# Graph network layers on one core: a memset behind every gather, and the next gather queued behind it

## The chip, the core and the metric

The kernel runs on one core of one Trainium2 chip. The metric is the device time of one launch in microseconds, as a median over runs without the profiler. A profile is one further execution, recorded by the hardware profiler; it takes longer than a plain run, as the table below shows.

## The reference

There are 12,500 nodes with 64 features and 400,000 edges, sorted by their target node `dst`. The first layer transforms nodes and edges and sums messages over the edges; the second multiplies twice by the normalised adjacency. Layer norms with residuals stand around both.

```python
x_t = mlp2(x, W1n, b1n, W2n, b2n)            # 12500 x 64
e_t = mlp2(edge_attr, W1e, b1e, W2e, b2e)    # 400000 x 64
msgs = x_t[src] * e_t * dp_scale
out = x + segment_sum(msgs, dst) * res_w
x = layernorm(x + norm(out) * gamma + beta)
# second layer: edges (src, dst) and self loops, weights deg^-1/2 on both ends
for _ in range(2):
    h = segment_sum(edge_weight * h[dst], src)
x = layernorm(x + h @ W.T + b)
```

## The kernel before

The edges are cut into 3125 chunks of 128 (one edge to a partition), and twelve chunks make a group `q`; there are 261 groups, taken from the last to the first.

Before the main loop the kernel computes `x_t` and stores it in the DRAM table `xt_tab`. For every group, `gathers` (L545) then issues one indirect DMA for each chunk from POOL (L553): it fetches the 128 rows `x_t[src]`, of 256 bytes each, into the tile `xg`. The pool of `xg` has four buffers, so gathers run up to four groups ahead of their use; a gather into a reused buffer waits until the product that read it is done. `load_ea` loads the edge features of the group over SP's queue.

Each group passes through these steps: `hidden` (L574, two products on PE, ScalarE and VectorE behind them), `message` (L588, L590 on PE, then the product with the gathered rows on VectorE, L598, in two halves), `level1` (L613, L623, L632: sums within the group) and `level2` (L642, L652: sums into a ring of node windows). `nodes` finishes windows of nodes with layer norms.

Beside this the same loop builds the adjacency as counts, in blocks: `adjacency` makes one-hot rows on VectorE (L795, L836), multiplies them on PE (L839), converts the sums on ScalarE (L853) and stores them (L862). Its edges come by indirect DMAs from POOL too (`fetch`, L738). `hop1` multiplies finished parts of the adjacency on PE (L1033, L1045, L1163).

After the loop comes the second hop. Part of it is dense on PE (L1138, L1149); the rest is sparse: POOL gathers rows (`sp_fetch`, L1357), PE multiplies them (L1375), and POOL scatters the sums by accumulating indirect DMAs into four tables (`sp_add`, L1388). POOL then adds the tables (L1515) and the last layer norm follows.

The order of instructions on each engine is set by a scheduler that simulates the timeline. The kernel gives it priorities: edge steps are traced at high priority, and pieces of adjacency and hop 1 are handed out between them in fixed shares. `tc.issue_after(ins)` adds an edge without a semaphore: what is traced in the block stands behind `ins` in its engine's queue.

Of the kernel before, what the change touches and what calls it, by code (L numbers as in the profile page):

```python
# [11 lines left out]
F32 = mybir.dt.float32  # L12
# [9 lines left out]
P = 128  # L22
# [162 lines left out]
def tile_fast(  # L185
# [42 lines left out]
    nc = tc.nc  # L228
    xt_tab = tc.dram_tile([NPAD, D], F32, name="xt_tab")
# [25 lines left out]
    CHK_SLOT, CHK_SG, CHK_Q = 2 * NSEG, 2 * NSEG + NSBP, 2 * NSEG + NSBP + len(SGS)  # L255

    const = ctx.enter_context(tc.tile_pool(name="const", bufs=1))
    main = ExitStack()
    idxp = main.enter_context(tc.tile_pool(name="idxp", bufs=2))
    xgp = main.enter_context(tc.tile_pool(name="xgp", bufs=4))  # L260
# [2 lines left out]
    with tc.tile_pool(name="srch", bufs=2) as srch, tc.tile_pool(  # L263
        name="srch1", bufs=1
# [40 lines left out]
        for k in range(NSBP):  # L305
            nc.gpsimd.indirect_dma_start(
                out=run[:, k, :],
                out_offset=None,
                in_=runs,
                in_offset=bass.IndirectOffsetOnAxis(ap=blki[:, k : k + 1], axis=0),  # L310
# [234 lines left out]
    def gathers(q):  # L545
        si, _ = seg[q // SEGQ]
        xg = xgp.tile([P, QC, D], F32, name="xg")
        real = min(QC, NCH - q * QC)
        if real < QC:
            nc.vector.memset(xg[:, real:, :], 0.0)  # L550
        for i in range(real):
            c = (q % SEGQ) * QC + i
            nc.gpsimd.indirect_dma_start(  # L553
                out=xg[:, i, :],
                out_offset=None,
                in_=xt_tab,
                in_offset=bass.IndirectOffsetOnAxis(ap=si[:, c : c + 1], axis=0),
            )
        xgs[q] = xg

    last_load = [None]

    def load_ea(q):
        t = eap.tile([P, SCC * P], F32, name="eat")
        last_load[0] = nc.sync.dma_start(t, ea[q]).ins
        eas[q] = t
# [620 lines left out]
    def take(q):  # L1187
        k = q // SEGQ
        if k not in seg:
            load_seg(k)  # L1190
        gathers(q)
        load_ea(q)
# [29 lines left out]
    for t in range(NQ + 3):  # L1222
# [18 lines left out]
        for f in units:  # L1241
# [3 lines left out]
            while a_live and a_spent < a_goal:  # L1245
                c = next(a_gen, None)
# [5 lines left out]
            while h_live and h_budget > 0:  # L1252
                try:
                    c = next(h_gen)
# [944 lines left out]
def build(nc, fast, general, params, out, **kw):  # L2199
    with tile.TileContext(nc, schedule_with_timeline_sim=True) as tc, ExitStack() as ctx:  # L2200
        fp = ctx.enter_context(tc.tile_pool(name="flag", bufs=1))
        flag = fp.tile([1, 1], I32, name="flag")
        tile_fast(tc, flag, *fast, *params, out, **kw)
        again = nc.values_load(flag, min_val=0, max_val=1)
        with tc.If(again > 0):
            tile_general(
                tc, *general, *params, out.rearrange("(p j) d -> p j d", j=NJ)
            )
# [27 lines left out]
```

## Time and profile before

| | before |
|---|---|
| median of 3 runs | 5303.93 us (5302.65 to 5309.74) |
| profiled execution | 7307.16 us, its span 7305.0 us |
| mean granted TensorE clock in the profile | 0.801 |
| PE busy | 5406.8 us, 74% of the span |
| VectorE busy | 3330.4 us, 46% |
| ScalarE busy | 2331.9 us, 32% |
| POOL busy | 3925.7 us, 54% |
| gathers (L553) | 3125, mean 1009 ns, from 93.0 to 6288.2 us |
| scatter-adds (L1388) | 389, mean 1558 ns, after the gathers |

Busy times are those of the profiled execution. A row of the costliest groups names the line, engine, operation, the tile written and those read, the count, busy time and the mean of one, and then the engine's idle time just before these instructions with what ended most of it. "issue" there means that the engine waited for nothing that the profile shows. A row of the timeline gives start and duration in microseconds, and in brackets the idle time before.

### The profile page before, as it was taken

The numbers are of one execution on the slowest core, as the hardware profiler recorded it, in microseconds if no ns is written. First come the engines' busy times: TensorE is split into PE (matmuls) and PEld (weight loads), VectorE is DVE, ScalarE is ACT, GpSimd is POOL, SyncE is SP. The second block draws the span as 40 slices with busy tenths as digits, with TensorE's granted clock in tenths as the row PEclk, the third lists the DMA queues.
The fourth block names the chain that finished last, engine by engine and source line by source line (L and its number), as shares of the span: only waits on it lengthen the run. The fifth ranks groups of instructions, "written<-read, shape, count | busy, mean of one in ns | idle before, by whom it ended". The sixth has DMA issues, their size and how long they took to land.

```text
span 7305.0 us, 91998 instructions
## 1 busy us (share of the span) xinstructions
PE 5406.8 (74%) x31510; PEld 2960.0 (41%) x31510; DVE 3330.4 (46%) x10617; ACT 2331.9 (32%) x7808; POOL 3925.7 (54%) x3677
## 2 busy tenths in 40 slices
PE   4666877778687776868777777787776776789992
PEld 2333443344343343434333334444344444534441
DVE  4545444545545545454454555555456543510003
ACT  1555444534433333333333343232222111210000
POOL 6555555554554544454444555555555454268885
PEclk6777888788788787778877888888788786599996
DMA  3534444434334333434343433333322222299884
GB/s 93 141 83 96 99 104 92 89 87 97 82 84 88 83 85 76 86 81 92 69 93 79 89 84 82 84 80 76 74 66 51 49 67 72 85 212 203 192 177 104
DMA packets 1258944, 698.98 MB, mean 96 GB/s; under 512 B 607516, under 2 KB 1191424, under 8 KB 1257440
## 3 DMA queue, kind: packets, MB, share of 16 engines
q1 hardware_dynamic: 1097552, 566.52, 31.2%
q0 software_dynamic: 160912, 126.49, 11.9%
q8 instruction: 249, 4.08, 0.2%
q14 instruction: 231, 1.89, 0.1%
HBM read 493.05 MB, written 199.62 MB: 95 GB/s over the span
## 4 chain that ended last, share of the span: by engine, by line
PE 60%; issue 12%; another core or an unknown queue 12%; DVE 5%; ACT 4%; POOL 4%; DMA 2%; SPq 0%; DVEq 0%; POOLq 0%; ACTq 0%
PE pa L839 15%; PE hacc_p L1033 10%; PE hacc_p L1045 6%; PE pw L574 6%; PE pe L590 5%; PE pl L623 5%; POOL hop_tab L1388 4%; PE pc L1163 3%; ACT stage L853 3%; PE acc L1138 3%; PE ring L652 2%; DVE oh L836 2%; PE pe L588 2%; PE acc L1149 1%
## 5 line engine op out<-in xcount | busy, mean ns | idle before, releaser
L553 POOL DMA_INDIRECT xg<-xt_tab,si x3125 | 3154.7, 1009 | 2995.7 <-issue 880.8
L836 DVE TENSOR_SCALAR oh<-iota_b,colT 128x391 bf16<-128x391 bf16 x6054 | 1707.7, 328 | 1710.0 <-PE pa L839 791.5
L853 ACT ACTIVATE stage<-pa 128x391 fp8e4<-128x391 f32 x3077 | 1507.9, 504 | 1930.0 <-PE pa L839 871.8
L839 PE MATMUL pa<-oh,koh 128*64 128x391 bf16 (+2 forms) x6054 | 1484.9, 410 | 726.7 <-issue 417.1
L839 PEld LDWEIGHTS <-koh 128*64 128x64 bf16 (+2 forms) x6054 | 718.7, 178 | 1188.6 <-issue 955.2
L1033 PE MATMUL hacc_p<-at,gp 128*128 128x512 fp8e4 (+1 forms) x2425 | 902.2, 432 | 202.6 <-ACT hev L1084 99.3
L1388 POOL DMA_INDIRECT hop_tab<-tot,first x389 | 605.9, 1558 | 119.4 <-issue 114.3
L574 PE MATMUL pw<-eat,w1ab 128*128 128x384 f32 x1044 | 545.3, 609 | 168.6 <-ACT z L575 85.6
L853 ACT ACTIVATION_READ_ACCUMULATOR stage<-pa 128x1 f32 x3077 | 642.4, 209 | 0.0
L1045 PE MATMUL hacc_p<-at,gp 128*64 128x512 fp8e4 (+1 forms) x2425 | 609.6, 448 | 10.5 <-issue 10.1
L590 PEld LDWEIGHTS pe<-w,z 128*128 128x128 f32 x3132 | 529.0, 230 | 123.7 <-issue 104.5
L590 PE MATMUL pe<-w,z 128*128 128x128 f32 x3132 | 553.5, 316 | 33.3 <-issue 33.1
L575 ACT ACTIVATE z<-pw,b 128x384 f32<-128x384 f32 x522 | 304.6, 584 | 628.8 <-remote 176.3
L623 PE MATMUL pl<-msg,oh 128*32 128x65 f32 x6264 | 419.1, 242 | 77.8 <-issue 65.0
L1045 PEld LDWEIGHTS <-gp 128*64 128x64 bf16 x2425 | 159.5, 113 | 780.3 <-issue 776.2
L652 PE MATMUL ring<-tot,oh 128*128 128x65 f32 x1096 | 205.5, 317 | 306.7 <-ACT tot L632 195.7
L1138 PE MATMUL acc<-at,gp 128*128 128x512 fp8e4 (+1 forms) x1900 | 429.6, 380 | 0.0
L623 PEld LDWEIGHTS pl<-msg,oh 128*32 128x32 f32 x6264 | 301.1, 120 | 236.5 <-issue 166.5
L598 DVE TENSOR_TENSOR msg<-pe,xg 128x384 f32<-128x384 f32 x522 | 287.9, 552 | 232.4 <-remote 107.0
L613 DVE TENSOR_TENSOR oh<-iota_f,rel 128x384 f32<-128x384 f32 x261 | 145.0, 556 | 539.5 <-remote 321.6
L1033 PEld LDWEIGHTS <-gp 128*128 128x128 bf16 x2425 | 179.5, 101 | 420.2 <-issue 399.0
L795 DVE TENSOR_TENSOR koh<-iota_k,keyT 128x1024 bf16<-128x1024 bf16 (+6 forms) x393 | 337.8, 860 | 0.0
(212 smaller groups left out, 4132.7 us busy)
## 6 DMA issues: line engine op xcount, KB each, us to landing
adj<-stage SPq DMA_DIRECT2D x390, 391.0 KB
at<-adj SPq DMA_DIRECT2D x97, 896.0 KB
at<-adj SPq DMA_DIRECT2D x144, 512.0 KB
eat<-in_eaq_dram SPq DMA_DIRECT2D x261, 192.0 KB
xg<-xt_tab,si POOLq DMA_INDIRECT x3125
at<-adj SPq DMA_DIRECT2D x120, 256.0 KB
at<-adj SPq DMA_DIRECT2D x24, 832.0 KB
at<-adj SPq DMA_DIRECT2D x24, 768.0 KB
```

What stands on the lines that cost most here:

```text
L553: nc.gpsimd.indirect_dma_start(out=xg[:, i, :], out_offset=None, in_=xt_tab, in_offset=bass.IndirectOffsetOnAxis(ap=si[:, c : c + 1], axis=0),
L574: nc.tensor.matmul(pw, w1ab[:, h, :], eas[q], start=True, stop=True)
L590: nc.tensor.matmul(pe[:, :, c, :], z[:, h, c * P : (c + 1) * P], w2, start=False, stop=(c == SCC - 1),)
L623: nc.tensor.matmul(pl[REL * s : REL * (s + 1), :], oh[:, s * SCC + c, :], m[:, s * SCC + c, :], start=(c == 0), stop=(c == SCC - 1), tile_ ...
L652: nc.tensor.matmul(ring[:, w % RING, :], oh[:, (w - lo) * P : (w - lo + 1) * P], tot, start=False, stop=False, skip_group_check=True,)
L836: nc.vector.tensor_scalar(oh, iota_b, colT[:, i % P : i % P + 1], None, op0=ALU.is_equal)
L839: nc.tensor.matmul(pa[rows, :], koh.pop(i), oh, start=(j == 0), stop=(j == caps[g] - 1), tile_position=(0, rows.start),)
L853: nc.scalar.activation(stage[:, u, :], pa, AF.Identity, saturate=True, accum_out=sums[:, u : u + 1],)
L1033: nc.tensor.matmul(acc[:, :w], gp[:kk, lo + i, 0:2, :].rearrange("p t d -> p (t d)"), t[:kk, i, :w], start=start, stop=False, skip_group_c ...
L1045: nc.tensor.matmul(acc[D * h : D * (h + 1), :w], gp[:kk, lo + i, 2, :], t[:kk, i, :w], start=False, stop=False, skip_group_check=True, til ...
L1138: nc.tensor.matmul(acc[:, :w], gp[:kk, wi, 0:2, :].rearrange("p t d -> p (t d)"), t[:kk, wi - lo, :w], start=first and n == 0, stop=False, ...
L1388: nc.gpsimd.indirect_dma_start(out=hop_tab[(q * QC + i) % HT], out_offset=bass.IndirectOffsetOnAxis(ap=first[:, q - Q0, i : i + 1], axis=0 ...
```

## The change

A tile `pause` of 128x128 f32 is added, which nothing reads. After every gather POOL sets it to zero. The memset is queued behind its gather, and the next gather behind the memset; other POOL work (the fetches) is not tied to it. The memsets all write one tile, so each also waits for the memset before it, on POOL's own semaphore.

```diff
     const = ctx.enter_context(tc.tile_pool(name="const", bufs=1))
+    pause = const.tile([P, P], F32, name="pause")
     main = ExitStack()
...
         for i in range(real):
             c = (q % SEGQ) * QC + i
-            nc.gpsimd.indirect_dma_start(
-                out=xg[:, i, :],
-                out_offset=None,
-                in_=xt_tab,
-                in_offset=bass.IndirectOffsetOnAxis(ap=si[:, c : c + 1], axis=0),
-            )
+            with tc.issue_after(last_pause[0]) if last_pause else ExitStack():
+                got = nc.gpsimd.indirect_dma_start(
+                    out=xg[:, i, :],
+                    out_offset=None,
+                    in_=xt_tab,
+                    in_offset=bass.IndirectOffsetOnAxis(ap=si[:, c : c + 1], axis=0),
+                ).ins
+            with tc.issue_after(got):
+                last_pause[:] = [nc.gpsimd.memset(pause, 0.0).ins]
         xgs[q] = xg
 
     last_load = [None]
+    last_pause = []
```

## The prediction

> **What bounds the kernel now.** I began with the page's busy shares and its forty slices, to see which engines are candidates and where the stages change; then the costliest groups; then POOL's timeline, because the edit touches POOL alone.
>
> ```profile
> PE 5406.8 (74%) x31510; PEld 2960.0 (41%) x31510; DVE 3330.4 (46%) x10617; ACT 2331.9 (32%) x7808; POOL 3925.7 (54%) x3677
> ...
> L553 POOL DMA_INDIRECT xg<-xt_tab,si x3125 | 3154.7, 1009 | 2995.7 <-issue 880.8
> L1388 POOL DMA_INDIRECT hop_tab<-tot,first x389 | 605.9, 1558 | 119.4 <-issue 114.3
> ```
>
> The first line makes POOL look half idle. The second says what its idle time is: before the 3125 gathers 2995.7 us pass, of which 880.8 us wait for nothing. The timeline shows that this part is a fixed price.
>
> ```profile
> 1024.42 0.94 POOL L553 DMA_INDIRECT xg<-xt_tab,si  x1 [0.30 <-issue]
> 1025.67 1.72 POOL L553 DMA_INDIRECT xg<-xt_tab,si  x1 [0.30 <-issue]
> 1027.70 0.94 POOL L553 DMA_INDIRECT xg<-xt_tab,si  x1 [0.30 <-issue]
> ...
> 1034.00 0.94 POOL L553 DMA_INDIRECT xg<-xt_tab,si  x1 [0.30 <-issue]
> 1043.64 1.01 POOL L553 DMA_INDIRECT xg<-xt_tab,si  x1 [8.70 <-DVE oh L836]
> ```
>
> Columns are start, duration, and in brackets the idle time before. Twelve gathers of a group follow each other with 0.30 us between them, never less; then POOL waits 8.70 us until an xg buffer is free. So a gather takes POOL 0.30 + 1.009 (its mean) = 1.31 us, and the rest of the 2995.7 us is waiting for buffers: in the profiled execution POOL has room.
>
> That room belongs to the profile. The profiled execution took 7307.16 us (span 7305.0), the median of the runs is 5303.93, so recording added 2003 us. It did not add it to POOL:
>
> ```profile
> 3000.73 0.94 POOL L553 DMA_INDIRECT xg<-xt_tab,si  x1 [0.30 <-issue]
> 3000.79 0.22 PE L623 MATMUL pl<-msg,oh 128*32 128x65 f32 x1 [1.18 <-issue]
> ...
> 3001.98 0.95 POOL L553 DMA_INDIRECT xg<-xt_tab,si  x1 [0.30 <-issue]
> ...
> 3003.62 0.38 PE L623 MATMUL pl<-msg,oh 128*32 128x65 f32 x2 [1.09 <-issue]
> ```
>
> PE, waiting for nothing, starts a small matmul only every 0.7 to 1.4 us, while POOL keeps its 1.25 us. The chain that ended last has 12% "issue" of this kind. So I add up POOL as if it never waited for a buffer: 93.0 us until the first gather; 3154.7 + 45.9 us busy in the 3125 gathers and 48 fetches (L738), and 3173 x 0.30 = 952 us between them, 4152 together; 140.3 us of handover before the first g4t (L1357); 875.5 us from there to the span's end, in which 389 scatter-adds run at 1.56 + 0.30 each with hardly a wait; 2.2 us outside the span. That is **5263 us, against a median of 5304**: 41 us of waiting are left. I read POOL as the bound without the profiler. PE is close behind: from back-to-back spacings in the timeline (six L839 products in 1.26 us, six L590 in 0.67, a pair each of L1033 and L1045 in 0.87, L574 0.8 each), its products up to the handover need about 3960 us, an estimate, 15.2 us per group of twelve chunks against POOL's 15.9. That two engines fit the median leaves room for error, which the range takes in.
>
> [...]
>
> **The change, part by part.**
>
> Nothing is removed and no DMA is added. Added are 3125 memsets of 128x128 f32 on POOL, one behind each gather. Each also waits for the memset before it (same tile, POOL's own semaphore); that one ended more than a gather earlier, so the wait should cost nothing. Queued behind each memset are the next gather, or an ed fetch, and whoever waits for those: msg L598 for xg, and the key preparation for ed.
>
> The price is in the start of the trace:
>
> ```profile
> 0.81 0.20 POOL masks.py:197 MEMSET ident<- 128x128 f32 x1 [0.29 <-POOLq L2216]
> 1.06 0.55 POOL L383 IOTA iota_i<- 128x512 int32 x1
> ```
>
> Same op, shape and type; start to next start is 1.06 - 0.81 = 0.25 us. I take **0.25 us** on top of the gather's 1.31, assuming the 0.30 gap remains. Sum: 3125 x 0.25 = 781 us; 5263 + 781 = **6044**, taken as 6040. Per group 12 x 0.25 = 3.0 us: POOL goes from 15.9 to 18.9, above PE's 15.2, so nothing takes the lead from POOL. Set against the profile's own time, the same 781 us fall into the 2996 - 952 = 2044 us of buffer waiting there, 7.8 us per group; a profile of the changed kernel may grow by only 0 to 400 us while the plain runs grow by 730. That cover isn't there without the profiler.
>
> What no row shows is the transition gather to memset to gather. Lower bound: the memset runs inside the 0.30 gap, 0; below nothing, if spacing the gathers also cured their delays, (1009 - 944) x 3125 = -203 us. Upper bound: a full 0.30 gap ahead of the memset too, 0.20 + 0.30 = 0.50[...]: 0.55, or 1719 us. I take 0.25 because tiny POOL instructions at the trace's start follow each other at 0.03 us, so a compute instruction does not itself need a 0.30 gap.
>
> Moved: the scheduler plans anew. In the order of PE's instructions more adjacency products (L839) now stand ahead of the early edge steps: before the 160th of 522 L574 products, 2047 instead of 1585 of 6054; POOL's first ed fetches come after 8 gathers instead of 20. Amounts are the same. With POOL slower this is the fitting order; splitting both orders into nine stretches and taking the slower of PE and POOL in each gives 685 us more instead of 781 at 18.9 against 15.9 per group. I keep 781 less a little, and count 41 us either way for the order. [...]
>
> **The rivals.**
>
> *Hidden in the gap.* [...] For it: memsets at 0.03 us spacing show overlapped dispatch. Against: the gap is as constant as a serial step. Time: 5304 with the order's 41 us either way; partly hidden (0.03 to 0.12 us) 5400 to 5680.
>
> *Switching costs on both sides.* 0.40 to 0.55 us each: 5263 + 1250 to 1719 = 6510 to 6980. For it: the constant gap at each gather. Against: nothing shows it for a memset.
>
> *Faster: spaced gathers stop stalling.* Place: gathers of 1.3 to 1.7 us such as the one at 1025.67, which with the mean cost 203 us in all. [...] It decides only when the memset adds under 0.065 us, so it needs the hidden case too: 5100 to 5290. Against: the scatter-adds run as closely at a steady 1.55.
>
> *POOL isn't the bound after all.* Were the 0.30 gap partly the profiler's, PE would set the time, and of 781 us only what exceeds POOL's slack would show: with 0.15 us less per gather (469 us slack), about 5620.
>
> **How the numbers follow.** Serial memset at 0.15 to 0.36 us, 5700 to 6400: 0.60, time 6040. Switching costs above that: 0.15. Partly hidden or PE-bound, 5315 to 5700: 0.11. Wholly hidden within 0.2% (some 11 us, about what a measurement of this kernel can tell): 0.04. Faster: 0.10. So slower 0.86. The range 5400 to 6750 leaves out the two last cases and the ends of two others, under 2 in 10.
>
> **What would show it.** A row of 3125 memsets near 204 ns on POOL; starts of gathers within a group 1.50 us apart, not 1.25; waiting for buffers before the gathers down by several hundred us; xg named as a releaser of L598 more often; the scatter stage unchanged at 1.86. Starts still 1.25 apart would make the forecast wrong, as would 1.50 apart with plain runs that don't lengthen: then POOL was not the bound.

## The result, and the profile after

The changed kernel takes 5592.91 us in the median (5589.85 to 5597.56, 4 runs) against 5306.84 us for the kernel before (4 runs): a ratio of 1.0538, with a 95% interval of 1.0519 to 1.0556. It is slower by 286 us, where some 736 us had been forecast (6040 less 5304).

The first recorded execution of the kernel before took 7307 us, and recording is not the reason: in one later job all eleven runs of that kernel took 7251 to 7361 us, for a cause that was not looked for, while its second recorded execution, the first experiment below, took 5328 us. So it does not hold here that a profile takes longer than a plain run, and what the change does is read from that second profile and the profile of the changed kernel.

The lines of the page of the changed kernel that answer to those shown of before (busy time and share, then the costliest groups on POOL, with line numbers shifted by the edit):

```profile
PE 4896.7 (88%) x31510; PEld 2774.8 (50%) x31510; DVE 3415.6 (61%) x10617; ACT 2279.8 (41%) x7808; POOL 4714.0 (84%) x6802
...
L555 POOL DMA_INDIRECT xg<-xt_tab,si x3125 | 3238.6, 1036 | 516.7 <-issue 494.8
...
L562 POOL MEMSET pause<- 128x128 f32 x3125 | 710.3, 227 | 1.5
L1393 POOL DMA_INDIRECT hop_tab<-tot,first x389 | 605.2, 1556 | 121.0 <-issue 113.7
```

The memsets are there, 3125 of them at 227 ns. The idle time before the gathers is 516.7 us, which is 0.165 us each, and 494.8 us of it is "issue": POOL hardly waits for a buffer. The scatter-adds (L1393) are as they were. The timeline of POOL shows the new step; the columns are start, duration and, in brackets, the idle time before:

```profile
1002.84 0.22 POOL L562 MEMSET pause<- 128x128 f32 x1
1003.22 0.95 POOL L555 DMA_INDIRECT xg<-xt_tab,si  x1 [0.16 <-issue]
1004.16 0.23 POOL L562 MEMSET pause<- 128x128 f32 x1
1004.55 1.01 POOL L555 DMA_INDIRECT xg<-xt_tab,si  x1 [0.16 <-issue]
1005.56 0.22 POOL L562 MEMSET pause<- 128x128 f32 x1
```

The memset begins as the gather ends, lasts 0.22 us, and the next gather begins 0.16 us after it. From the end of one gather to the start of the next pass 0.38 us, where the kernel before has 0.30. The memset does not come on top of the gap; it lies in it and lengthens it by 0.08 us (from 0.305 to 0.381 us in the median of all gathers of the two traces).

### The profile page after: what moved, and what is told of

It reads as the page before. It is cut to its first block, busy times and chain, and to the rows that moved or that the text cites. A ratio compares the mean times of both kernels' runs of the same rounds, so it can differ in the third digit from the quotient of the medians.

```text
span 5593.3 us, 95026 instructions
## 1 busy us (share of the span) xinstructions
PE 4896.7 (88%) x31510; PEld 2774.8 (50%) x31510; DVE 3415.6 (61%) x10617; ACT 2279.8 (41%) x7808; POOL 4714.0 (84%) x6802
## 4 chain that ended last, share of the span: by engine, by line
POOL 42%; PE 33%; DVE 9%; issue 8%; DMA 5%; ACT 2%; SPq 0%; DVEq 0%; POOLq 0%; ACTq 0%
POOL xg L555 27%; POOL hop_tab L1393 7%; PE pa L844 7%; PE hacc_p L1038 6%; POOL pause L562 6%; DVE oh L841 5%; PE hacc_p L1050 4%; DMA xg<-xt_tab,si 3%; PE pe L595 3%; PE pl L628 3%; PE acc L1143 2%; PE pw L579 2%; PE pc L1168 2%; ACT stage L858 1%; PE acc L1154 1%
## 5 line engine op out<-in xcount | busy, mean ns | idle before, releaser
L555 POOL DMA_INDIRECT xg<-xt_tab,si x3125 | 3238.6, 1036 | 516.7 <-issue 494.8
L841 DVE TENSOR_SCALAR oh<-iota_b,colT 128x391 bf16<-128x391 bf16 x6054 | 1818.6, 355 | 322.4 <-PE pa L844 317.1
L844 PE MATMUL pa<-oh,koh 128*64 128x391 bf16 (+2 forms) x6054 | 1267.2, 367 | 126.4 <-DVE oh L841 39.5
L1038 PE MATMUL hacc_p<-at,gp 128*128 128x512 fp8e4 (+1 forms) x2425 | 794.0, 392 | 26.1 <-ACT hev L1089 24.2
L562 POOL MEMSET pause<- 128x128 f32 x3125 | 710.3, 227 | 1.5
L1393 POOL DMA_INDIRECT hop_tab<-tot,first x389 | 605.2, 1556 | 121.0 <-issue 113.7
L579 PE MATMUL pw<-eat,w1ab 128*128 128x384 f32 x1044 | 488.3, 551 | 49.0 <-ACT z L580 42.6
L1050 PE MATMUL hacc_p<-at,gp 128*64 128x512 fp8e4 (+1 forms) x2425 | 524.6, 410 | 0.0
L595 PE MATMUL pe<-w,z 128*128 128x128 f32 x3132 | 487.4, 297 | 0.0
L582 DVE SCALAR_TENSOR_TENSOR z<-z 128x768 f32<-128x768 f32 x261 | 247.5, 948 | 279.8 <-ACT z L580 279.5
L593 PE MATMUL pe<-b2p,ones_b 128*128 128x384 bf16 x522 | 185.6, 356 | 205.5 <-DVE msg L603 190.0
```

The source lines that it names most:

```text
L555: got = nc.gpsimd.indirect_dma_start(out=xg[:, i, :], out_offset=None, in_=xt_tab, in_offset=bass.IndirectOffsetOnAxis(ap=si[:, c : c + 1] ...
L562: last_pause[:] = [nc.gpsimd.memset(pause, 0.0).ins]
L579: nc.tensor.matmul(pw, w1ab[:, h, :], eas[q], start=True, stop=True)
L595: nc.tensor.matmul(pe[:, :, c, :], z[:, h, c * P : (c + 1) * P], w2, start=False, stop=(c == SCC - 1),)
L841: nc.vector.tensor_scalar(oh, iota_b, colT[:, i % P : i % P + 1], None, op0=ALU.is_equal)
L844: nc.tensor.matmul(pa[rows, :], koh.pop(i), oh, start=(j == 0), stop=(j == caps[g] - 1), tile_position=(0, rows.start),)
```

## The experiments

Theory A: POOL never waits in the main loop, so its step per gather sets the time; the memset costs only the time by which it lengthens the gap between two gathers. Rivals: the new plan makes the difference (B), switching between memset and gather has a fixed price (C), the memset costs wherever it runs (D), and, tried last, it costs even where POOL has room, by disturbing VectorE (E).

**The kernel before, recorded again.** No edit.

> The kernel before, unchanged, to get a second profiled execution of it. Theory A (POOL is the bound without the stretched recording): if this execution is not stretched like the first one, its span is about 5305 us, the gathers run from about 80 to 4320 us with 1.25 us or more between starts, and waiting for a free xg buffer before the gathers is under 150 us in all. Rival B (PE or the plan sets the time, POOL has room): a span of about 5305 us as well, but several hundred us of buffer waiting before the gathers.

Measured: 5327.94 us, one execution. Its page's busy line, and its POOL groups:

```profile
PE 4784.6 (90%) x31510; PEld 2738.1 (51%) x31510; DVE 3313.9 (62%) x10617; ACT 2316.4 (43%) x7808; POOL 4022.3 (76%) x3677
```

```profile
L553 POOL DMA_INDIRECT xg<-xt_tab,si x3125 | 3250.9, 1040 | 954.0 <-issue 877.4 <-DMA xg<-xt_tab,si 30.5 <-DVE oh L836 26.5
```

The idle time before the gathers is 954.0 us against 2995.7 in the first profile, and 3125 gaps of 0.305, the median, make 953 of it. Buffer waiting has gone, as theory A has it. The gathers start between 77.7 and 4343.5 us. PE's busy share, 90%, is the higher one all the same: what tells the bound is that POOL waits for next to nothing, while PE is idle for 298 of the 4220 us from 80 to 4300 us.

**One column instead of 128.**

```diff
-                last_pause[:] = [nc.gpsimd.memset(pause, 0.0).ins]
+                last_pause[:] = [nc.gpsimd.memset(pause[:, :1], 0.0).ins]
```

> The memset behind each gather clears one column (128x1) instead of 128. Theory A with the overlap seen in the changed kernel (after a memset the gap to the next gather is 0.16 us instead of 0.30, and the memset starts as the gather ends): the step is 0.95 + about 0.11 + 0.16 = 1.22 us against 1.245, so the time is 5307 - 3125 x 0.03 = about 5220 us (5180 to 5290), below the kernel before. Rival B (the plan or a disturbed PE or VectorE makes the 286 us): the plan stays close to that of the changed kernel, so 5450 to 5600 us. Rival C (a fixed price for each switch between gather and memset): about the same 0.09 us as before, 5550 to 5600 us.

Measured: 5330.03 us, ratio 1.0044 (1.003 to 1.0059). This is none of the three forecasts, though nearest to A's upper end. C falls: there are as many switches as before the edit, and 260 us are gone. B does not fall with this run, for the plan moved too: of the 6054 adjacency products on PE, 1651 now stand ahead of the 160th of the 522 L574 products, where the kernel before has 1585 and the changed kernel 2047. The timeline says why no time was gained:

```profile
1003.18 1.36 POOL L555 DMA_INDIRECT xg<-xt_tab,si  x1 [0.19 <-issue]
1004.54 0.11 POOL L562 MEMSET pause<- 128x1 f32 x1
1004.85 0.94 POOL L555 DMA_INDIRECT xg<-xt_tab,si  x1 [0.19 <-issue]
```

0.11 + 0.19 makes 0.30 again: the gather starts 0.30 us after the end of the gather before, as if there were no memset. This holds even behind a memset that takes longer:

```profile
101.05 1.03 POOL L555 DMA_INDIRECT xg<-xt_tab,si  x1 [0.19 <-issue]
102.07 0.38 POOL L562 MEMSET pause<- 128x1 f32 x1
102.38 0.94 POOL L555 DMA_INDIRECT xg<-xt_tab,si  x1
```

This memset is recorded as ending at 102.45, after the next gather has begun. So the traces show two limits. A gather starts 0.30 us after the end of the gather before and no sooner (0.303 us is the smallest gap in the first trace of before). Behind a memset of 128 columns it also starts no sooner than some 0.16 us after the memset's end (0.154 at the least, 0.162 in the median of the changed kernel's trace), which makes the step 0.95 + 0.22 + 0.16; the one-column memsets in these rows, of 0.11 and 0.38 us, don't hold it back. Why the slow one doesn't stays open. The 19 us that this run took more than before do not come from this gap; part of them may lie in POOL's `ed` fetches, whose idle time is 33.4 us here and 14.6 in the second profile of before.

**256 columns.**

```diff
-    pause = const.tile([P, P], F32, name="pause")
+    pause = const.tile([P, 2 * P], F32, name="pause")
```

> The memset clears 256 columns instead of 128. Theory A: from the first trace a memset column costs about 0.9 ns (128 columns 0.20 us, 1 column 0.10 us), so the memset takes about 0.33 us, the gap after it stays 0.16, and 3125 x 0.11 = 340 us come on top of 5593: about 5930 us (5850 to 6000). Rival B: well under 340 us more, since POOL has room. Rival C: 5593 us within 1%.

Measured: 5892.42 us, ratio 1.1103 (1.1084 to 1.1121): 299 us above the 128-column memset, close to the 340 expected under A.

```profile
L562 POOL MEMSET pause<- 128x256 f32 x3125 | 1045.7, 335 | 1.5
```

The memset is 108 ns longer than at 128 columns, and 108 x 3125 = 338 us; the mean gather was 13 ns shorter in this run (1023 ns against 1036), which takes off 41. What the memset gained in length shows in the time.

**The queueing without the memset.**

```diff
-            with tc.issue_after(got):
-                last_pause[:] = [nc.gpsimd.memset(pause, 0.0).ins]
+            last_pause[:] = [got]
```

> No memset at all; each gather is only queued behind the gather before it, which they were in practice already. Theory A: 5307 us within 0.3%, gathers 1.25 us apart. Rival B (the queueing edges and the plan that follows from them make the change): 5400 to 5600 us.

Measured: 5309.67 us, ratio 0.9995 (0.9982 to 1.0007). The queueing edges alone cost nothing. They don't test the plan: PE's instructions come in the same order here as in the kernel before.

**Behind every second gather.** Of the twelve gathers of a group, those with an odd number have no memset.

```diff
+            if i % 2:
+                last_pause[:] = [got]
+                continue
             with tc.issue_after(got):
```

> The 128-column memset behind every second gather only, six to a group. Theory A (POOL never waits, so each memset adds its net step of 0.09 us: 0.22 of memset plus a gap of 0.16 in place of 0.30): half of the 282 us, 5311 + 141 = about 5450 us (5430 to 5475). Rival B (the time comes from the new plan): near 5593 or near 5311, not halfway.

Measured: 5457.56 us, ratio 1.0278 (1.0261 to 1.0295), 146 us more than before: half of 286. In its timeline both steps stand side by side:

```profile
999.42 0.95 POOL L555 DMA_INDIRECT xg<-xt_tab,si  x1 [0.16 <-issue]
1000.67 0.94 POOL L555 DMA_INDIRECT xg<-xt_tab,si  x1 [0.30 <-issue]
1001.61 0.22 POOL L565 MEMSET pause<- 128x128 f32 x1
1001.99 0.95 POOL L555 DMA_INDIRECT xg<-xt_tab,si  x1 [0.16 <-issue]
```

Starts are 1.25 us apart without and 1.32 with a memset between, within one execution. The plan, too, lies about halfway (1831 adjacency products where before has 1585 and the changed kernel 2047), so the time alone doesn't tell A from B; the run with two memsets below does.

**The memset on VectorE.** In the kernel before, with the tile `pause` added, behind each gather:

```diff
+            nc.vector.memset(pause, 0.0)
```

> 3125 memsets of the same tile, but issued on VectorE, one traced behind each gather; POOL's program is that of the kernel before. Theory A (it is POOL's time that counts): 5311 us within 1%, since VectorE is busy 62% and gets some 500 us more at most. Rival D (what counts is the memset as such, its writes or its semaphores beside the other work): 5450 to 5600 us.

Measured: 5289.0 us, ratio 0.9964 (0.9953 to 0.9975). VectorE spent 515.6 us more in these memsets and the kernel was, if anything, quicker. D falls: the same memset, 165 ns each there, cost nothing on VectorE.

**Two memsets of one column.**

```diff
+                nc.gpsimd.memset(pause[:, :1], 0.0)
-                last_pause[:] = [nc.gpsimd.memset(pause, 0.0).ins]
+                last_pause[:] = [nc.gpsimd.memset(pause[:, 1:2], 0.0).ins]
```

> Two memsets of one column behind each gather. Model: the step is the gather's 0.95 us plus the larger of 0.30 and (memsets + 0.17 to 0.19). If the second memset overlaps the first as the tiny ones at the start of the trace do (0.03 us apart), the step grows by 0.02 to 0.03: 5311 + 60 to 100 = about 5390 us. If each takes its 0.12 us in turn, the step grows by 0.12: 5311 + 375 = about 5690 us. Rival C (the whole price is that of switching from a memset to a gather): 5330 us, as with one.

Measured: 5355.99 us, ratio 1.0089 (1.007 to 1.0107), 45 us more than before. This is under the 60 to 100 us expected for two that overlap.

```profile
1000.83 0.12 POOL L562 MEMSET pause<- 128x1 f32 x1
1000.86 0.11 POOL L563 MEMSET pause<- 128x1 f32 x1
1001.14 1.04 POOL L555 DMA_INDIRECT xg<-xt_tab,si  x1 [0.16 <-issue]
```

The two overlap, their starts 0.03 us apart, and end 0.14 to 0.15 us after the gather; with 0.16 that is 0.30. Over the whole trace the median from the end of a gather to the start of the next is 0.305 us, as without a memset, so the step has not grown. The 45 us arise elsewhere. The first row below has POOL's `ed` fetches in the second profile of before, the second row has them in this run:

```profile
L738 POOL DMA_INDIRECT ed<-in_edges_dram,startI x48 | 47.6, 991 | 14.6 <-issue 14.3 <-DMA xg<-xt_tab,si 0.3
L744 POOL DMA_INDIRECT ed<-in_edges_dram,startI x48 | 59.8, 1246 | 57.3 <-DVE oh L842 44.6 <-issue 12.7
```

The fetches wait 43 us longer, mostly for VectorE, and take 12 us more. The new plan, in which the first fetch comes after 8 gathers instead of 20, may be the reason; no run tests that.

This run also settles how much B can explain. Its order of PE's instructions is almost that of the run with a memset behind every second gather (1801 and 1831 adjacency products ahead of the 160th L574 product; over all 522 the two differ by 11 in the mean), and yet the times differ by 102 us. The plan can hardly make that difference. The gap can: it is 0.305 us here and 0.381 behind each of the 1563 memsets there, and 1563 x 0.076 = 119 us. So B falls as the main cause. Some tens of us, as here, may still come from the plan.

**Ten gathers of twelve.** The last two gathers of every group are left out.

```diff
-        if real < QC:
-            nc.vector.memset(xg[:, real:, :], 0.0)
+        real = min(real, QC - 2)
+        nc.vector.memset(xg[:, real:, :], 0.0)
```

> The last two gathers of every group are left out and their columns cleared by VectorE, so those messages are zero; all else stays. POOL loses 521 gathers of 1.34 us, 698 us. Theory A (POOL is the bound and PE some way below it): the time falls by 300 to 650 us, to 4660 to 5010, depending on where PE sets in. Rival B (PE and POOL are equally tight): it falls by less than 150 us, to above 5160.

Measured: 5271.4 us, ratio 0.9928 (0.9911 to 0.9944). That is what rival B of this run said, not A: 700 us less work on POOL saves 40 us, and buffer waiting is back.

```profile
L553 POOL DMA_INDIRECT xg<-xt_tab,si x2605 | 2693.9, 1034 | 1340.6 <-issue 709.7 <-DVE oh L836 354.4 <-DVE msg L598 95.1
```

So POOL was the bound by some 40 us only, and the next bound stands right below it. PE is the likely one, though no run tests it. The busy times of the engines from 80 to 4300 us follow (PE, weight loads, VectorE, ScalarE, POOL, then clock, DMA share and GB/s), first in the second profile of before, then here:

```profile
80.00:4300.00 4220.00, 3921.63 (x25098) 2283.87 (x25099) 3087.07 (x10142) 2189.88 (x7545) 3261.46 (x3141) 0.95 0.58 122
80.00:4300.00 4220.00, 4012.87 (x25407) 2276.16 (x25408) 3152.90 (x10455) 2235.95 (x7573) 2745.51 (x2652) 0.95 0.55 119
```

PE's busy time rises from 3922 to 4013 of the 4220 us. That the next bound is so near matters in one direction only: shortening POOL's step gains little, lengthening it costs in full.

**The change with ten gathers of twelve.** Both edits together.

> The change as it is (128 columns on POOL), with the last two gathers of every group and their memsets left out as in the run of ten of twelve. POOL needs 2604 x 1.42 = 3700 us in the main loop, PE about 4190. Theory A (a memset costs time only where POOL is the bound): 5271 us within 0.7%, since POOL still has room. Rival E (a memset costs its 0.09 us wherever it is, because it disturbs VectorE and so PE): 5271 + 2604 x 0.09 = 5505 us.

Measured: 6359.99 us, in the job in which the kernel before took 7298.91 (ratio 0.8698, 0.8656 to 0.874). That can't be set beside 5271, so it was run again.

> The same kernel as in the run before last (the change, with the last two gathers of every group and their memsets left out), which ran where the kernel before itself took 7299 us and so can't be set beside 5271. Theory A: 0.993 of the kernel before, as without the memsets, within 0.007 (5235 to 5310 us if that is at 5311). Rival E (a memset costs 0.09 us even where POOL has room): 1.037 of it, 5505 us.

Measured: 5249.75 us against 5301.64, ratio 0.9898 (0.9876 to 0.9919).

```profile
L555 POOL DMA_INDIRECT xg<-xt_tab,si x2605 | 2741.0, 1052 | 619.2 <-issue 403.6 <-DVE oh L841 141.8 <-DVE msg L603 48.2
...
L562 POOL MEMSET pause<- 128x128 f32 x2605 | 602.1, 231 | 1.2
```

With 2605 memsets in it the kernel is no slower than without them (ratio 0.9898 against 0.9928); 2605 x 0.083, some 216 us, were at stake. The same memset is free as soon as POOL has room, so E falls and A holds.

**One column on VectorE.** This asks whether the 22 us that the VectorE memset took off came from the plan or from the time VectorE spends in it.

> The memset on VectorE again, with one column instead of 128. If the 22 us that the 128-column one took off came from the plan that follows from 3125 more VectorE instructions, this one takes off 10 to 40 us as well (5270 to 5300). If they came from the time VectorE spends in them[...], it takes off less than half of that: 5300 to 5315.

Measured: 7380.21 us, in the same job as the 6359.99 us, where the kernel before took 7298.91 (1.0111, 1.0078 to 1.0145); run again:

> One column on VectorE, as before, again because the last one ran where the kernel before took 7299 us. If the plan makes the gain: 0.992 to 0.998 of the kernel before; if the time spent in the 128-column memset does: 0.998 to 1.001.

Measured: 5307.55 us against 5301.64, ratio 1.0015 (1.0007 to 1.0023), just above the second forecast. Merely having 3125 more VectorE instructions doesn't bring the gain. The mean gather took 1020 ns with 128 columns on VectorE and 1035 with one. Whether the time that VectorE spends in the longer memset makes gathers quicker, or its plan does, which differs from that of before and of the one-column run, stays open.

## Why the prediction was wrong

The sign and the bound held. POOL set the time, the memset lies on its path step by step, nothing else took the lead, and the scatter stage did not change. What failed was one term of the sum.

**The term.** "I take 0.25 us on top of the gather's 1.31, assuming the 0.30 gap remains." It did not remain: 0.22 of memset and 0.16 of gap replace 0.30, which is 0.08 us in place of 0.25. In means over the whole stage: (3238.6 + 516.7 + 710.3) / 3125 = 1.429 us per gather in the changed kernel, (3250.9 + 954.0) / 3125 = 1.346 in the second profile of before. The difference of 0.083 us x 3125 = 261 us is most of the 286 (and of the 268 by which the two profiled spans differ), where the prediction had 781.

**What replaced it.** The first rival, "partly hidden (0.03 to 0.12 us)", described the event; it was given a chance of about one in ten and a time of 5400 to 5680. The reason given for serial execution, that tiny POOL instructions at the trace's start follow each other at 0.03 us, was read the wrong way round. Those memsets last 0.10 to 0.12 us each, so one started while another was at work, and that speaks for work in the gap: the runs with one and two memsets of one column show that some 0.14 us of memset fits into it without lengthening the step. What the trace of before could not show is how long the gap is between a memset and an indirect DMA. "Switching costs on both sides", in whose upper end of 0.55 us the last 0.05 were an estimate that no run tests, fell with the timeline, in which the memset starts right as the gather ends.

**The room in the first profile.** "So recording added 2003 us" was wrong: the second recorded execution took 5327.94 us, where the runs of its job lay between 5297.62 and 5329.29. That this room had no bearing on the plain runs was right, and the second profile confirms it with hardly any room at all. That the sum of POOL's work came so near, 5263 us against 5304, was partly luck. In the second profile the gathers are busy for 3250.9 us, 96 more than in the sum, and the time ahead of the first gather and after the last one is 50 us shorter; the "41 us of waiting" that were left are not there.

**PE close behind.** Forecast at 15.2 us per group against POOL's 15.9; the run with ten gathers found the next bound 40 us, or 0.15 us per group, below POOL, not 0.7. The prediction used PE only to say that it would not take over when POOL slows, and that held. "POOL isn't the bound after all" fell with the second profile.

**Spaced gathers** hardly stalled less: the mean gather was 1036 ns against 1040.

**VectorE beside the memsets.** One row of VectorE moved with the memset on POOL. Columns are as in the costliest groups; first the second profile of before, then 128 and 256 columns of memset:

```profile
L836 DVE TENSOR_SCALAR oh<-iota_b,colT 128x391 bf16<-128x391 bf16 x6054 | 1719.9, 336 | 509.3 <-PE pa L839 493.7 <-PE hacc_p L1045 2.2
```

```profile
L841 DVE TENSOR_SCALAR oh<-iota_b,colT 128x391 bf16<-128x391 bf16 x6054 | 1818.6, 355 | 322.4 <-PE pa L844 317.1
```

```profile
L841 DVE TENSOR_SCALAR oh<-iota_b,colT 128x391 bf16<-128x391 bf16 x6054 | 1987.8, 384 | 270.3 <-PE pa L844 265.0 <-PE pw L579 0.2
```

The same VectorE instruction gets longer, 336, 355, 384 ns, as POOL's memset does. But the memset's length is not all: with one column the row has 340 ns, and with two memsets of one column, together 0.15 us, it has 358. What makes it longer no run tests. VectorE had room for the longer instructions: it was busy for 61% of the span with 128 columns and with 256.

## What to carry to other kernels

Before pricing an instruction that is put between two others, ask how much of it can run in the gap that already lies between those two: here the work first filled that gap, and only the rest was paid. An engine that hardly ever waits can be the bound even at 76% busy, if fixed gaps fill the rest of its main loop; count them into its step. And a bound with a second one 40 us below it is lopsided: here adding to it cost in full, and taking from it gained almost nothing. Last, an edit can change the scheduler's plan: before calling the plan ruled out, look for two runs with nearly the same plan.

## What the runs showed of the hardware

- Between two indirect DMAs on POOL lie 0.30 us (the gathers of before: 0.305 in the median, 0.303 at the least). From the end of a memset of 128 or 256 columns to the next indirect DMA lie 0.16 us, and a memset starts right as the DMA ends (1.5 us of idle time before 3125 memsets). A memset of one column, or two of them that end 0.14 to 0.15 us after the gather, fit into the 0.30 us without lengthening it.
- A memset on POOL over 128 partitions takes 129, 227 and 335 ns in the mean for 1, 128 and 256 f32 columns: by these three, 0.77 to 0.84 ns per column and 0.12 to 0.13 us fixed. On VectorE it took 59 ns for one column and 165 for 128. The starts of two memsets of one column on POOL lie 0.03 us apart.
